# Attention over compacted tokens: when the first checks and loads run, and the order of the last product

## The chip, the core and the metric

The kernel runs on one core of a Trainium2 chip (trn2). The metric is device time in microseconds (us) of one execution, as the median of several runs. The engines are TensorE (PE, with its weight loads listed as PEld), VectorE (DVE), ScalarE (ACT), GpSimd (POOL) and SyncE (SP). In this kernel SP issues the plain transfers and POOL the indexed ones: gathers of token rows and scatters of result rows.

## The reference

The input `x` is 16 batches of 512 features by 1024 tokens, `mask` is 16 by 1024 of zeros and ones (about half are ones), `Wq` and `Wo` are 512 by 512.

```python
xt = transpose(x)                       # B, T, D
q = xt @ Wq.T                           # 8 heads of 64; queries are keys and values too
scores = scale * einsum('bhqd,bhkd->bhqk', qh, qh)
logits = (scores * cmask + (1.0 - cmask) * NEG) * rmask
attn = softmax(logits)
ctx = einsum('bhqk,bhkd->bhqd', attn, qh)
out = x + transpose(ctx @ Wo.T)
```

A token whose mask is 0 has a row of zero logits, so it attends to all tokens equally and its context is the mean of `q`. A token whose mask is 1 attends only to tokens whose mask is 1.

## The kernel before

The fast path works on compacted tokens. For each batch `slots` and `index` compute, from the mask, the list of the unmasked tokens, and POOL gathers their rows into `C` = 544 slots: four blocks of 128 (`xa`) and a tail of 32 (`xt`). The tails of some batches are collected, so that a group of batches shares one product for them. The masked tokens get one row per batch, the mean of `q` times `Wo`, added to their `x`.

Products that need more precision than one f16 are made of two halves. A value is scaled and split into `h` and `l` (f16), and three products `h*h`, `l*h`, `h*l` are added up. `xsplit` makes `xh` and `xl` of the transposed tokens, `split` makes `wqh`, `wql`, `woh`, `wol` of the weights, `qsplit` makes `hl` of the queries. `qsplit` then spreads these halves over the partitions by four SP transfers (L442 to L445) into `xx`, the operand of the scores.

For one batch the work is: transposes of the tokens (L398) and their splits (L358 ACT, L359 DVE); 8 query products (L421, four chunks `e` by two column halves `g`, 12 matmuls each) and their copies by ACT (L424); the spread into `xx`; transposed values (L467, L469); a shift for the exponentials, from the largest square norm of a head's queries (`top`, L505 to L511, and `bottom`, L518 to L532, whose result is `nm`); scores (L580, and L555 for the tails), exponentials on ACT (L584, L559), products with the values (L598, L601), a copy `c` (L605), reciprocal sums (L620 to L639) that go through DRAM and come back spread as `rb`, `norm` (L665 to L671) and the output product (L681). The result is added to the gathered rows (L686) and scattered by POOL (L765).

The sums of all tokens that the mean needs come from the natural layout. `load_half` (batches 0 and 1, 256 KB each) and `load_all` (the others, 512 KB each) load rows of `x_nat`, and `sum_half` (L343) sums them on ACT. For the first two batches the halves are put into buffers called `xm`, `ub` and `xi`.

The fast path is only valid for numbers in range. `range_x` (L366, one reduction for each chunk of `xh`, and L368) and `range_w` (L373, one reduction over all of `wqh` or `woh`) put the largest sizes into `big`, and `ranges` compares them at the end (L379 to L386). Nothing else reads them.

The order is set in two ways. `run` writes the program: a list `first` for the start of batch 0, then for each batch 18 steps of scores, between which a list `m` of other work (with costs that only set where an item goes) and lists `free` by step are laid. The framework then orders each engine's instructions when the program is built. `behind(i)` asks it to put what follows after instruction `i`. `once(dma, after)` makes a transfer wait for an instruction. Each engine, and each issuing queue, works through its own list in order. `self.st[0]["top"]` is the last reduction of the first shift (L523), that is, what the first exponentials of the kernel subtract. PSUM has two buffers for scores (`ps_s`), one for the values' product and two for everything else (`pm`).

`last` makes the output product of the last batch. Its three first chunks of features do not need the last `norm`; the fourth (`range(3, DC)`) does. `pos[0]` to `pos[3]` are the four blocks of 128 slots, `pos[4]` is the product of the tails.

Of the kernel before, what the change touches and what calls it, by code (L numbers as in the profile page):

```python
# [12 lines left out]
F16 = mybir.dt.float16  # L13
I32 = mybir.dt.int32
AF = mybir.ActivationFunctionType
ALU = mybir.AluOpType
AX = mybir.AxisListType
PS = bass.MemoryType.PSUM

P = 128  # L20
# [5 lines left out]
DC = D // P  # L26
# [5 lines left out]
CT = C - 512  # L32
# [17 lines left out]
class Fast:  # L50
# [78 lines left out]
    def setup2(self):  # L129
        nc, fixed = self.nc, self.fixed  # L130

        self.quad = fixed("quad", [P, HG])
        nc.vector.tensor_reduce(self.quad, self.ident.rearrange("p (r t) -> p r t", r=HG), AX.X, ALU.add)
        self.xh = fixed("xh", [P, DC, CQ], F16)
        self.xl = fixed("xl", [P, DC, CQ], F16)
        for t in (self.xh, self.xl):
            nc.gpsimd.memset(t[:, :, CM + 1:], 0.0)

        self.rcol = [fixed("rcol%d" % k, [P, P]) for k in range(2)]
        self.smcol = [fixed("smcol%d" % k, [P, P]) for k in range(2)]  # L140
        for t in self.rcol + self.smcol:
            nc.gpsimd.memset(t, 0.0)

        self.big = fixed("big", [P, self.B + 2])

        self.par = fixed("par", [P, 2])
        nc.vector.tensor_tensor(self.par, self.quad[:, 0:2], self.quad[:, 2:4], ALU.add)
# [194 lines left out]
        with self.behind(*self.exp):  # L342
            self.nc.scalar.activation(s["xm"][k], s["xm"][k], AF.Copy, accum_out=s["ms2"][:, k:k + 1])  # L343

    def load_all(self, b, c):

        t = self.sb([P, T], F32, "xm", 2)
        self.nc.sync.dma_start(out=t, in_=self.x_nat[b, c * P:(c + 1) * P, :])
        self.st[b]["xm"].append(t)

    def xsplit(self, dst, src, scaled=False):
# [15 lines left out]
        if c == DC - 1:  # L367
            nc.vector.tensor_reduce(self.big[:, b:b + 1], s["top4"], AX.X, ALU.max)  # L368

    def range_w(self, name):  # L370
        wh = self.w[name][0]
        k = self.B + "qo".index(name)
        self.nc.vector.tensor_reduce(self.big[:, k:k + 1], wh, AX.XY, ALU.max, apply_absolute_value=True)  # L373

    def ranges(self):

        nc, B = self.nc, self.B
        ok = self.sb([P, B + 2], F16, "okr")
        nc.vector.tensor_scalar(ok[:, :B], self.big[:, :B], XMAX, None, ALU.is_le)  # L379
        nc.vector.tensor_scalar(ok[:, B:], self.big[:, B:], WMAX, None, ALU.is_le)  # L380
        pe = self.pm([P, B + 2])
        nc.tensor.matmul(pe, lhsT=self.on16, rhs=ok, start=True, stop=True)
        least = self.sb([P, 1], F32, "okl")
        nc.vector.tensor_reduce(least, pe, AX.X, ALU.min)
        nc.vector.tensor_scalar(least, least, float(P), None, ALU.is_equal)
        nc.vector.tensor_scalar(self.ok, self.ok, least, None, ALU.mult)  # L386
# [388 lines left out]
    def last(self, b, todo):  # L775

        for f in self.soon + todo:
            f()
        self.soon = []
        while self.urgent or self.spare:  # L780
            self.issue()
        self.paced = False
        s = self.st[b]
        self.recip(b, 3)
        pos = []
        for i in range(2):
            t = self.ps_s.tile([P, 2, D], F32, tag="s", name="pss")
            pos += [t[:, k, :] for k in range(2)]
        pos.append(self.pm([P, D]))
        for i in range(4):  # L790
            self.product(s["ch"], s["cl"], slice(i * P, (i + 1) * P), pos[i], range(3))
        self.norm(b, 3)
        tails = slice(0, len(self.group[b]) * CT)
        self.product(*s["ct"], tails, pos[4], range(1))
        for i in range(4):
            if i == 2:
                self.product(*s["ct"], tails, pos[4], range(1, 3))
            self.project(b, i, pos[i], range(3, DC))
        self.project_tail(b, pos[4], range(3, DC))

    def run(self, flag):
        B = self.B
        L = lambda f, *a: lambda: f(*a)
# [5 lines left out]
        def xt(n):  # L809
            return [(0.45, L(self.xt, n, c)) for c in range(4)] + [(0.25, L(self.xt, n, 4))]  # L810

        def query(n, e, g):
            u = [(1.37, L(self.query, n, e, g))]
            return u + [(0, L(self.qsplit, n, e))] if g else u

        def value(n, e):
            return [(0.45, L(self.value, n, e))]
# [7 lines left out]
        tails, rests = {}, {}  # L825
# [39 lines left out]
        first = query(0, 0, 0) + xt(0)[3:] + [(0, L(self.facts, 0, 2))] + query(0, 1, 0) + query(0, 0, 1)  # L865
        first += [(0, index1)] + value(0, 0) + g1[:1] + query(0, 1, 1)[:1] + g1[1:2]
        first += [(0, L(self.split, "q", c, 1)) for c in range(DC)]
        first += [(0, lambda k=k: self.load_half(1, k, self.last_xt)) for k in range(2 * DC)]
        first += value(0, 1) + [(0, L(self.value_tail, 0, 0))] + query(0, 2, 0) + g1[2:3] + query(0, 2, 1)[:1] + g1[3:4]
        first += [(0, L(self.sum_half, 1, k)) for k in range(3)] + [(0, shift0)]  # L870
        for _, f in first:
# [1 line left out]
        with self.behind(self.st[0]["top"]):  # L873
            for _, f in query(0, 1, 1)[1:] + query(0, 2, 1)[1:]:
                f()
        self.paced = True
        begin = g1[4:] + [(1.5, lambda: None)] + query(0, 3, 0) + value(0, 2) + query(0, 3, 1) + value(0, 3)
        begin += [(0.3, L(self.value_tail, 0, 1)), (0, L(self.means, 0))]
        begin += [(0, L(self.load, "o", c)) for c in range(DC)]
        begin += [(0, L(self.range_x, 0, c)) for c in range(DC)] + [(0, L(self.range_w, "q"))]  # L880
        groups = [(g, min(h, B)) for g, h in ((2, 4), (4, 8), (8, 12), (12, 16)) if g < B]
        todo, ready, whole = [], [], []
        for b in range(B + 1):
            o, n = b - 1, b + 1
# [3 lines left out]
            free, early, late = {}, ([], []), []  # L888
# [13 lines left out]
            if n < B:  # L902
                m = xt(n)[:1] + early[0] + xt(n)[1:2] + chunk2 + xt(n)[2:3] + early[1] + xt(n)[3:] + tp + query(n, 0, 0) + query(n, 0, 1) + bt + value(n, 0)
# [13 lines left out]
            else:  # L917
# [7 lines left out]
                m = chunk2 + early[0] + early[1] + tp + bt + [(2.6, L(self.project_means, b))] + late + P_(0, 1, 2, 3)  # L925
# [3 lines left out]
                if b == g[0] - 2:  # L929
                    m.insert(7 if b == 0 else 0, (0.1, L(self.slots, *g)))  # L930
            if b == 1:
                m.append((0, L(self.range_w, "o")))
            if b == B - 1:
                m.append((0.1, self.ranges))
            if b == 0:
                m = begin + m
            if b + 2 < B:
                self.start(b + 2)
                for c in range(DC):
                    at = 3 * c + (0 if b else 4)  # L940
                    free.setdefault(at, []).append(L(self.load_all, b + 2, c))
                    free.setdefault(at + 4, []).append(L(self.sum_half, b + 2, c))
            if b == 0:
                for k in range(3, 2 * DC):
                    free.setdefault(k // 2, []).append(L(self.sum_half, 1, k))
            total = sum(c for c, _ in m)
            done, pos = 0.0, 0
            for st, (p, i) in enumerate(S):
# [20 lines left out]
                big = st >= 4 and [c >= 1 for c, _ in fill if c > 0.1][:1] == [True]  # L969
# [166 lines left out]
```

## Time and profile before

| | |
|---|---|
| Median of 3 runs | 1118.86 us (1118.13 to 1123.56) |
| Profiled execution, its own time | 1119.63 us |
| Its span, first to last instruction | 1117.8 us |
| PE / DVE / ACT / POOL busy | 1071.0 / 731.6 / 676.8 / 288.6 us |
| Mean granted TensorE clock | 0.996 |
| DMA, mean over the span | 162 GB/s |
| Idle before ACT's exponentials L584, for scores | 209.6 us |
| Idle before DVE's `norm` L665, for `rb` | 48.4 us |

The table is of one profiled execution, except its first row. Busy time of PE is modelled at the ends of matmuls, so it is somewhat too long. Idle time of an engine other than the one that sets the pace costs nothing; the prediction therefore goes to the stretches in which PE waits.

### The profile page before, as it was taken

Reading aid. Unit: us, or ns where it says so; the run is one execution under the profiler, and the core shown is the slowest. Engines: PE = TensorE matmul, PEld = TensorE weight load, DVE = VectorE, ACT = ScalarE, POOL = GpSimd, SP = SyncE. Lnnn points to the kernel's source line nnn. Section 1 sums busy time; section 2 is a strip of 40 time slices with the busy share of each in tenths; the row PEclk is TensorE's granted clock in tenths of the full one; section 3 lists DMA queues with packets and bytes.
Section 4 is the critical chain, followed back from the end, with each engine's and each line's share of the span. In section 5 each row is a group of like instructions: output and inputs, shape, how many; then the busy total and the mean of one; then the engine's idle time right before and its main releaser. Section 6 shows DMA issues by size and latency. Waiting matters only on the chain.

```text
span 1117.8 us, 23184 instructions
## 1 busy us (share of the span) xinstructions
PE 1071.0 (96%) x8386; PEld 697.7 (62%) x8386; DVE 731.6 (65%) x2369; ACT 676.8 (61%) x1716; POOL 288.6 (26%) x303
## 2 busy tenths in 40 slices
PE   7899999999999999999999999999999999998987
PEld 6576666666666666566666666666666666665543
DVE  6787466765665767667665766857576685655543
ACT  5876666666566666567565665666566666645540
POOL 3101031323202222222222232222222223214542
PEclk9999999999999999999999999999999999999999
DMA  7745455646546464565655566465656654546652
GB/s 235 212 121 155 128 164 150 190 127 185 144 128 177 125 209 142 163 179 159 192 145 173 158 185 182 130 193 146 198 157 176 185 146 146 147 115 194 187 168 72
DMA packets 78121, 181.34 MB, mean 162 GB/s; under 512 B 15008, under 2 KB 16800, under 8 KB 78000
## 3 DMA queue, kind: packets, MB, share of 16 engines
q1 hardware_dynamic: 56816, 111.62, 36.4%
q0 software_dynamic: 21184, 68.18, 19.2%
q8 instruction: 68, 1.11, 0.4%
q14 instruction: 53, 0.43, 0.1%
HBM read 92.34 MB, written 33.91 MB: 113 GB/s over the span
## 4 chain that ended last, share of the span: by engine, by line
PE 63%; DVE 14%; DMA 10%; issue 7%; ACT 3%; POOL 2%; SPq 1%; DVEq 0%; POOLq 0%; ACTq 0%
PE pav L598 17%; PE pss L580 16%; PE pm L681 13%; PE pm L421 8%; DMA xi<-x_in,idx 3%; DMA rb<-rd 2%; PE pm L398 2%; PE pav L601 2%; DMA rd<-rr 2%; ACT p L584 2%; POOL y_out L765 2%; PE pm L467 1%; DVE c L665 1%; PE pm L634 1%; DVE tmp L458 1%
## 5 line engine op out<-in xcount | busy, mean ns | idle before, releaser
L584 ACT ACTIVATE p<-pss,nm 128x544 f32<-128x544 f32 x512 | 363.8, 715 | 219.9 <-PE pss L580 209.6
L580 PE MATMUL pss<-xx 128*128 128x272 f16 x2048 | 303.1, 280 | 5.4 <-DMA xx<-hl 2.6
L598 PE MATMUL pav<-p,v 128*64 128x272 f32 x2048 | 278.9, 402 | 0.9 <-ACT c L605 0.9
L580 PEld LDWEIGHTS <-xx 128*128 128x128 f16 x2048 | 192.4, 99 | 85.2 <-issue 40.2
L598 PEld LDWEIGHTS pav<-p,v 128*64 128x64 f32 x2048 | 131.0, 136 | 98.2 <-issue 38.5
L765 POOL DMA_INDIRECT y_out<-xa,idx x68 | 70.9, 1043 | 304.8 <-PE pss L580 163.6
L421 PE MATMUL pm<-xh,wqh 128*128 128x274 f16 (+1 forms) x512 | 143.7, 281 | 0.1
L421 PE MATMUL pm<-xl,wqh 128*128 128x274 f16 (+1 forms) x512 | 143.2, 280 | 0.2 <-DVE xl L359 0.2
L421 PE MATMUL pm<-xh,wql 128*128 128x274 f16 (+1 forms) x512 | 143.2, 280 | 0.0
L313 POOL DMA_INDIRECT xa<-x_in,idx x68 | 69.3, 1020 | 181.7 <-PE pss L580 89.8
L421 PEld LDWEIGHTS <-wqh 128*128 128x128 f16 x1024 | 99.7, 99 | 23.1 <-issue 4.7
L584 ACT ACTIVATION_READ_ACCUMULATOR p<-pss,nm 128x1 f32 x512 | 102.9, 201 | 0.0
L686 DVE SCALAR_TENSOR_TENSOR xa<-pm,xa 128x512 f32<-128x512 f32 x60 | 41.4, 689 | 87.1 <-PE pm L681 87.0
L313 POOL DMA_INDIRECT xi<-x_in,idx x60 | 59.7, 995 | 145.7 <-PE pss L580 49.0
L424 ACT ACTIVATE q<-pm 128x272 f32<-128x272 f32 (+1 forms) x128 | 51.2, 400 | 69.0 <-PE pm L421 68.7
L681 PE MATMUL pm<-woh,ch 128*128 128x512 f16 x240 | 91.1, 380 | 1.0 <-DVE xa L686 1.0
L681 PE MATMUL pm<-woh,cl 128*128 128x512 f16 x240 | 91.0, 379 | 0.0
L681 PE MATMUL pm<-wol,ch 128*128 128x512 f16 x240 | 90.9, 379 | 0.0
L765 POOL DMA_INDIRECT y_out<-xi,idx x60 | 60.3, 1004 | 89.6 <-PE pss L580 70.6
L665 DVE TENSOR_TENSOR c<-c,rb 128x544 f32<-128x544 f32 x64 | 46.3, 724 | 54.7 <-DMA rb<-rd 48.4
L681 PEld LDWEIGHTS <-ch 128*128 128x128 f16 x480 | 46.3, 98 | 41.8 <-issue 1.2
L752 DVE TENSOR_TENSOR xi<-xi,ub 128x512 f32<-128x512 f32 (+1 forms) x60 | 40.1, 687 | 40.6 <-DMA xi<-x_in,idx 27.7
(191 smaller groups left out, 1584.7 us busy)
## 6 DMA issues: line engine op xcount, KB each, us to landing
xx<-hl SPq DMA_DIRECT2D x256, 136.0 KB
xm<-x_nat_in SPq DMA_DIRECT2D x56, 512.0 KB
rb<-rd SPq DMA_DIRECT2D x128, 136.0 KB
pt<-c SPq DMA_DIRECT2D x64, 136.0 KB
pt<-p SPq DMA_DIRECT2D x64, 136.0 KB
ub<-ud SPq DMA_DIRECT2D x16, 256.0 KB
xi<-x_nat_in SPq DMA_DIRECT2D x8, 256.0 KB
xa<-x_in,idx POOLq DMA_INDIRECT x68, 4.3
```

The lines of the kernel that those rows point to most:

```text
L313: dma = self.nc.gpsimd.indirect_dma_start(out=tile[:n], out_offset=None, in_=self.x, in_offset=bass.IndirectOffsetOnAxis(ap=idx, axis=0))
L398: self.pe = nc.tensor.transpose(pt[:, c, :], x[:n, c * P:(c + 1) * P], self.ident[:n, :n]).ins
L421: self.beat = nc.tensor.matmul(pq, lhsT=w[:, c, e * P:(e + 1) * P], rhs=xx[:, c, cols], start=(k == 0), stop=(k == 3 * DC - 1)).ins
L424: nc.scalar.activation(s["q"][:, e, cols], pq, AF.Copy, scale=1.0 / (SX * SW))
L580: self.beat = nc.tensor.matmul(pt[:, g, :CH], lhsT=xx[:, 2 * k, i * P:(i + 1) * P], rhs=xx[:, 2 * k + a, g * CH:(g + 1) * CH], start=(a == ...
L584: self.exp = [nc.scalar.activation(t.rearrange("p (g c) -> p g c", g=2), pt[:, :, :CH], AF.Exp, bias=s["nm"][p // HG][:, p % HG:p % HG + 1 ...
L598: nc.tensor.matmul(s["pav"][k * DK:(k + 1) * DK, g, :CH], lhsT=s["v"][p][:, i, k * DK:(k + 1) * DK], rhs=ps[k][:, cols], start=(i == 1), s ...
L665: nc.vector.tensor_tensor(c, c, s["rb"][p], ALU.mult)
L681: nc.tensor.matmul(po[:cols.stop - cols.start], lhsT=a[:, e, cols], rhs=w[:, e, :], start=(e == 0 and k == 0), stop=(e == DC - 1 and k == 2))
L686: self.nc.vector.scalar_tensor_tensor(x, po, 1.0 / (SX * SW), x, ALU.mult, ALU.add)
L752: self.nc.vector.tensor_tensor(x[:n], x[:n], s["ub"][:n], ALU.add)
L765: dma = self.nc.gpsimd.indirect_dma_start(out=self.out, out_offset=bass.IndirectOffsetOnAxis(ap=idx, axis=0), in_=x, in_offset=None)
```

## The change

The change moves work, and removes none.

- `range_x` of batch 0 and `range_w` of `Wq` are put behind the first shift. `range_w` now makes one reduction for each chunk of 512 columns instead of one for all four, so `big` and `ok` have six more columns.
- The halves 4 to 7 of batch 1 (four transfers of 256 KB), the four loads of `Wo` (256 KB each) and the first loads of batch 2 (512 KB each) wait for the first shift. Which step the sums of batch 1 are laid into changes with them (`k // 3` for `k // 2`).
- In `last`, the product of the tails is written behind the four blocks, not between them.

```diff
-        self.big = fixed("big", [P, self.B + 2])
+        self.big = fixed("big", [P, self.B + 2 * DC])
...
-    def load_all(self, b, c):
+    def load_all(self, b, c, after=None):
...
-        self.nc.sync.dma_start(out=t, in_=self.x_nat[b, c * P:(c + 1) * P, :])
+        self.once(self.nc.sync.dma_start(out=t, in_=self.x_nat[b, c * P:(c + 1) * P, :]), after)
...
-    def range_w(self, name):
-        wh = self.w[name][0]
-        k = self.B + "qo".index(name)
-        self.nc.vector.tensor_reduce(self.big[:, k:k + 1], wh, AX.XY, ALU.max, apply_absolute_value=True)
+    def range_w(self, name, c):
+
+        k = self.B + DC * "qo".index(name) + c
+        self.nc.vector.tensor_reduce(self.big[:, k:k + 1], self.w[name][0][:, c, :], AX.X, ALU.max, apply_absolute_value=True)
...
-        tails = slice(0, len(self.group[b]) * CT)
-        self.product(*s["ct"], tails, pos[4], range(1))
         for i in range(4):
-            if i == 2:
-                self.product(*s["ct"], tails, pos[4], range(1, 3))
             self.project(b, i, pos[i], range(3, DC))
-        self.project_tail(b, pos[4], range(3, DC))
+        self.project_tail(b, pos[4])
...
-        first += [(0, lambda k=k: self.load_half(1, k, self.last_xt)) for k in range(2 * DC)]
+        first += [(0, lambda k=k: self.load_half(1, k, self.last_xt)) for k in range(DC)]
...
+        first_top = self.st[0]["top"]
+
+        def apart(f, *a):
+            def run():
+                with self.behind(first_top):
+                    f(*a)
+            return run
...
-        begin += [(0, L(self.load, "o", c)) for c in range(DC)]
-        begin += [(0, L(self.range_x, 0, c)) for c in range(DC)] + [(0, L(self.range_w, "q"))]
+        begin += [(0, L(self.load, "o", c, None, first_top)) for c in range(DC)]
+        begin += [(0, apart(self.range_x, 0, c)) for c in range(DC)] + [(0, apart(self.range_w, "q", c)) for c in range(DC)]
...
-                m.append((0, L(self.range_w, "o")))
+                m += [(0, L(self.range_w, "o", c)) for c in range(DC)]
...
-                    free.setdefault(at, []).append(L(self.load_all, b + 2, c))
+                    free.setdefault(at, []).append(L(self.load_all, b + 2, c, None if b else first_top))
...
                 for k in range(3, 2 * DC):
-                    free.setdefault(k // 2, []).append(L(self.sum_half, 1, k))
+                    if k >= DC:
+                        free.setdefault(0, []).append(lambda k=k: self.load_half(1, k, first_top))
+                    free.setdefault(k // 3, []).append(L(self.sum_half, 1, k))
```

More of the change, by code (lines that the diff above doesn't have):

```diff
@@ L368, in range_x @@
             nc.vector.tensor_reduce(self.big[:, b:b + 1], s["top4"], AX.X, ALU.max)
-    def range_w(self, name):
-        wh = self.w[name][0]
-        k = self.B + "qo".index(name)
-        self.nc.vector.tensor_reduce(self.big[:, k:k + 1], wh, AX.XY, ALU.max, apply_absolute_value=True)
+    def range_w(self, name, c):
+        k = self.B + DC * "qo".index(name) + c
+        self.nc.vector.tensor_reduce(self.big[:, k:k + 1], self.w[name][0][:, c, :], AX.X, ALU.max, apply_absolute_value=True)
     def ranges(self):
         nc, B = self.nc, self.B
-        ok = self.sb([P, B + 2], F16, "okr")
+        ok = self.sb([P, B + 2 * DC], F16, "okr")
         nc.vector.tensor_scalar(ok[:, :B], self.big[:, :B], XMAX, None, ALU.is_le)
         nc.vector.tensor_scalar(ok[:, B:], self.big[:, B:], WMAX, None, ALU.is_le)
-        pe = self.pm([P, B + 2])
+        pe = self.pm([P, B + 2 * DC])
         nc.tensor.matmul(pe, lhsT=self.on16, rhs=ok, start=True, stop=True)
```

## The prediction

> **What bounds the kernel now.** I read the page first, then two-microsecond windows and the engines' timelines at the two places that the change touches: the start of batch 0 and the last product.
>
> ```profile
> PE 1071.0 (96%) x8386; PEld 697.7 (62%) x8386; DVE 731.6 (65%) x2369; ACT 676.8 (61%) x1716; POOL 288.6 (26%) x303
> ```
>
> TensorE is busy 96% of the span. Only its idle time, 47 us in all, can be won, and only where the change touches it. The windows (PE, PEld, DVE, ACT, POOL busy, clock, DMA share, GB/s) show where it idles near the start:
>
> ```profile
> 24.00:26.00 2.00, 1.73 (x16) 1.31 (x13) 2.00 (x5) 1.53 (x3) 0.74 (x1) 1.00 0.98 348
> 26.00:28.00 2.00, 1.01 (x5) 0.45 (x6) 2.00 (x5) 1.01 (x3) 0.94 (x1) 1.00 1.04 367
> 30.00:32.00 2.00, 0.93 (x8) 0.54 (x6) 2.00 (x2) 2.00 (x8) 1.24 (x2) 1.00 0.86 198
> 32.00:34.00 2.00, 0.62 (x4) 0.32 (x4) 0.61 (x3) 0.16 (x2) 0.64 (x1) 1.00 0.94 339
> 46.00:48.00 2.00, 0.93 (x7) 0.65 (x7) 2.00 (x5) 2.00 (x6) 0.00 (x0) 1.00 0.03 7
> ```
>
> DVE is full up to 32 while the DMA engines are full too; at 46 ACT and DVE are full and PE waits. VectorE's timeline names what fills it, and what comes behind (start, duration, line, output<-input, idle before):
>
> ```profile
> 22.36 0.71 DVE L366 TENSOR_REDUCE top<-xh 128x1 f32<-128x545 f16 x1
> 24.53 0.71 DVE L366 TENSOR_REDUCE top<-xh 128x1 f32<-128x545 f16 x1
> 26.83 1.34 DVE L366 TENSOR_REDUCE top<-xh 128x1 f32<-128x545 f16 x2
> 29.70 2.28 DVE L373 TENSOR_REDUCE big<-wqh 128x1 f32<-128x2048 f16 x1
> 32.45 0.15 DVE L507 TENSOR_TENSOR smcol<-smcol,sdt 128x4 f32<-128x4 f32 x1
> 35.80 0.16 DVE L520 TENSOR_SCALAR nm<-pm 128x4 f32<-128x4 f32 x1 [0.54 <-PE pm L518]
> ```
>
> The five range checks stand before the shift `nm` of the first exponential. The chain of waits, PE's and ACT's timelines show the second thing that is late, the spread query halves `xx`:
>
> ```profile
> 28.00 6.07 DMA xx<-hl
> 30.65 0.28 PE L421 MATMUL pm<-xh,wql 128*128 128x274 f16 x1
> 33.18 0.62 PE L580 MATMUL pss<-xx 128*128 128x272 f16 x4 [2.25 <-DMA xx<-hl]
> 34.20 0.62 PE L580 MATMUL pss<-xx 128*128 128x272 f16 x4 [0.40 <-DMA xx<-hl]
> 36.00 0.71 ACT L584 ACTIVATE p<-pss,nm 128x544 f32<-128x544 f32 x1 [3.83 <-DVE nm L520]
> ```
>
> The end is a row of five scatters on POOL, 1.2 to 1.3 us apart, then the last landing:
>
> ```profile
> 1106.20 0.96 POOL L765 DMA_INDIRECT y_out<-xa,idx  x1 [12.43 <-DVE xa L686]
> 1107.93 0.96 POOL L765 DMA_INDIRECT y_out<-xa,idx  x1 [0.78 <-DVE xa L686]
> 1109.23 0.96 POOL L765 DMA_INDIRECT y_out<-xa,idx  x1 [0.35 <-DVE xa L686]
> 1110.50 0.90 POOL L765 DMA_INDIRECT y_out<-xg,tails  x1 [0.31 <-issue]
> 1111.71 0.96 POOL L765 DMA_INDIRECT y_out<-xa,idx  x1 [0.30 <-issue]
> ```
>
> **The change, part by part.** I take the order on each engine from the two built programs, and durations from the rows.
>
> *Checks off VectorE.* The four L366, L368 and L373 leave the stretch 22-32. The first two L366 stand where other waits cover part of them: squares end on ACT at 25.52, so `sd` (L459) moves from 26.01 only to 25.55. From there the chain value-transpose, L487, L492 moves by 0.5; L373 goes whole, so L507 comes at about 29.7 instead of 32.45. On PE the two small products for the shift (L509, L518) now stand among the last query matmuls, not behind the eight score matmuls: L511 about 30.2, L520 about 31.0 (before 35.80), the "first largest score" L523 about 31.4 (36.20).
>
> *Loads behind that score.* Four of the eight 256 KB halves of batch 1 (k 4 to 7), the four `wo` loads (256 KB each) and the first 512 KB loads of batch 2 wait on SP for L523. So `xx` of chunk 0 has 1.05 MB less ahead of it: 3.0 us at the 348 to 367 GB/s of 24-28. Its first spread can issue at 25.3 (25.91), the fourth about 27.4. When does it land? The row says 6.07 us from issue. [...] I take 30.0, since half of the backlog goes and the DMA share stays near 1 till then.
>
> *First scores.* Then PE's own matmuls end last: scores start at 31.1 and PE has these eight, L509 and L518 behind it at 32.0 instead of 35.62: **-3.6 us**. ACT must first do the query copy L424 and `corr`, so the first exponential is at 32.1 instead of 36.00.
>
> *From there to batch 1's first query (58.92).* New: two sums of halves (k 4, 5; L343, pitch 0.61) stand on ACT ahead of the fourth exponential, and their transfers are issued at 31.6 and 32.2. With two gathers, 1.05 MB at 350 GB/s, they land about 35.5. Queued behind them on ACT is the exponential that frees a score buffer for PE: **+1.8** (1.2 if landed early, 2.5 if late). Gone: the old waits at 38.9 and 39.65, 0.22 and 0.40. Also the four splits of `wo` (L162, pitch about 0.53, 2.1 us) leave ACT before 49, where PE waited 0.53, 0.56 and 0.37 for exponentials: I count **-1.3** of these 1.46. Sum of the start: -3.6 + 1.8 - 0.6 - 1.3 = **-3.7 us**. Bounds: 5.8 if all 2.2 us of later idle time goes too; 1.7 if `xx` lands at 33.4 and the lead at the first scores is all there is. [...]
>
> *What is moved later and costed at nothing.* The spreads of chunk 1 wait behind two halves on SP, but their data is ready at 33.1 (38.07) and PE needs them about 38; they land about 37.8. The checks of `xh` and `wq` fall in DVE's idle stretches after 33 (2.51 idle before 41.61); each L373 becomes four, 0.63 each by L366's pitch, so 0.3 us more a weight, 0.6 in all. The `wo` splits (L163), its checks and ACT's L162 move to 55-75, where DVE had waits of 1.03, 0.73, 0.41, 0.97 and 0.78 and ACT one of 2.93, while PE ran without a gap. If that cover is gone, up to 2 us come back. `wo` is first multiplied at 116.83. POOL's order is untouched but for the last two scatters; its `xt` gather merely starts earlier. From 60 to the tail the order is the same and PE nearly full, so the lead is carried to the end.
>
> *The tail.* With the tails' product last, the first output block needs no three tail matmuls ahead (0.77 us): its addition is at 1104.4 (1105.23), its scatter at 1105.4 (1106.20). PE waits for no one, so POOL sets the pace: four more at 1.26 give 1110.4 for the last (1111.71). The tail addition is ready at 1109.7, hidden by 0.7. The last scatter carries 64 rows, not 128: another 0.3 by the 274 GB/s of 1113-1114. Together **-1.6** (0.8 if only the first scatter moves, 2.0 at most).
>
> Sum: -3.7 - 1.6 = -5.3. Against the profiled execution's 1119.63 this gives 1114.3. The median is 0.77 lower, so I predict **1113.6**, or -0.47%.
>
> **The rivals.**
>
> *The lead is lost at ACT.* The sums wait for halves that now come late, and exponentials queue behind them. For it: ACT had not a gap from 36 to 54. Against: DMA is nearly idle from 44 to 48 and only 1 MB is ahead. If it eats 2 to 3.5 of the 3.7, the tail and a rest remain: 1115.6 to 1117.1.
>
> *All idle time goes.* ACT, relieved, runs ahead and the later waits vanish: -5.8 (my upper bound) to -6.8 (all that the windows show idle from 22 to 58) at the start: 1110.5 to 1111.5. Against: the new ACT wait is in the program's order.
>
> *Slower: `wo` comes too late.* Its loads now stand on SP behind the spreads of chunks 1 to 3 and the `pt` copies. ACT's L162 stands between exponentials of batch 0 and would block them, and VectorE's L163 blocks `nm` of the second half. I expect SP to issue `wo` about 45.5 to 47.5, landed by 50, and L162 reached at 57. It decides from a landing at 57; each microsecond later costs PE one: beyond 62 the kernel is slower than before, beyond 68 by over 0.5%. At 69 it stands at 1125. Against: seven microseconds of margin.
>
> That the change does nothing is excluded at the tail, where the order plainly differs.
>
> **How the numbers follow.** Forecast 0.66, own range 1111.6 to 1115.6; ACT loses the lead 0.17; all idle goes 0.09; slower 0.08. One half of a percent, 5.6 us, is about what a measurement can tell from no change: the line is at 1113.3, almost through my forecast. Faster: 0.30 of the forecast plus 0.09 = 0.39. Same: 0.36 plus 0.17 = 0.53. Slower 0.08. Range 1110.5 to 1118.1: from the second rival's end to the whole lead lost with the tail at its lower bound (1118.86 - 0.8); the slower rival is left out.
>
> **What would show it.** Right: L520 near 31, first L580 near 31 with no wait for `xx`, first L584 near 32, batch 1's first L421 near 55, the last scatter carrying `xg`, some 5 us before 1111.71. Wrong: a wait for `xx` still ending after 33, an ACT wait for `xi` over 3 us, an ACT or DVE wait for `wo`, or a lead at 60 that has gone by 120.

## The result, and the profile after

The changed kernel took 1115.4 us (median of 18 runs, 1109.8 to 1118.9) beside 1121.1 us for the kernel before on the same chip: ratio 0.995, 95% interval 0.9934 to 0.9965, which is 5.6 us less. Predicted were 5.3 us less: 1113.6, counted from 1118.86 for the kernel before; in these runs that kernel itself took 2.2 us more. A second series of the same kernel gave 0.9939 (0.9918 to 0.996).

The profiled execution took 1115.95 us with a span of 1114.2. The page, VectorE's timeline at the first shift, PE's at the first scores, ScalarE's from the first exponential, and SP's issues there (start, duration, line, output<-input, idle before and its releaser):

```profile
PE 1071.4 (96%) x8386; PEld 699.1 (63%) x8386; DVE 732.3 (66%) x2375; ACT 676.9 (61%) x1716; POOL 290.8 (26%) x303
```
```profile
31.64 0.16 DVE L507 TENSOR_TENSOR smcol<-smcol,sdt 128x4 f32<-128x4 f32 x1
33.05 0.16 DVE L520 TENSOR_SCALAR nm<-pm 128x4 f32<-128x4 f32 x1 [0.48 <-PE pm L518]
```
```profile
32.99 1.09 PE L580 MATMUL pss<-xx 128*128 128x272 f16 x8
36.92 0.29 PE L555 MATMUL pss<-xx 128*32 128x272 f16 x2
40.35 0.28 PE L555 MATMUL pss<-xx 128*32 128x272 f16 x1 [2.88 <-DMA xx<-hl]
```
```profile
34.03 0.71 ACT L584 ACTIVATE p<-pss,nm 128x544 f32<-128x544 f32 x1
37.27 0.63 ACT L343 ACTIVATE xi<-xi 128x512 f32<-128x512 f32 x1 [0.45 <-DMA xi<-x_nat_in]
39.20 0.63 ACT L343 ACTIVATE xi<-xi 128x512 f32<-128x512 f32 x1 [1.20 <-DMA xi<-x_nat_in]
39.82 0.69 ACT L584 ACTIVATE p<-pss,nm 128x544 f32<-128x544 f32 x1
```
```profile
33.67 0.91 SPq L337 DMA_DIRECT2D xi<-x_nat_in  x2
35.20 0.47 SPq L442 DMA_DIRECT2D xx<-hl  x1
35.76 0.55 SPq L443 DMA_DIRECT2D xx<-hl  x1
```

These times can't be set beside those of before as they stand. The first query matmul of the second block, which the change doesn't reach, came at 19.93 us before and at 21.72 here. It is taken as the zero below. On that scale the shift L520 moved from 15.9 to 11.3, the first exponential from 16.1 to 12.3, and the 2.25 us that PE waited for `xx` at its first scores are gone. A new wait stands 7 us behind the first scores: the third L555, the first matmul to read chunk 1 of `xx`, waits 2.88 us. The windows (PE, PEld, DVE, ACT, POOL busy, clock, DMA share, GB/s) show it, with the DMA engines full, and show the later waits closed:

```profile
32.00:34.00 2.00, 2.00 (x17) 1.57 (x18) 1.20 (x8) 1.64 (x7) 0.72 (x2) 1.00 0.33 89
38.00:40.00 2.00, 0.00 (x0) 0.00 (x0) 1.69 (x3) 0.81 (x3) 0.00 (x0) 1.00 1.01 238
46.00:48.00 2.00, 2.00 (x17) 1.30 (x16) 1.78 (x8) 2.00 (x7) 0.00 (x0) 1.00 0.37 83
```

The end, on POOL:

```profile
1102.29 0.96 POOL L765 DMA_INDIRECT y_out<-xa,idx  x1 [11.55 <-DVE xa L686]
1106.09 0.96 POOL L765 DMA_INDIRECT y_out<-xa,idx  x1 [0.31 <-issue]
1107.36 0.91 POOL L765 DMA_INDIRECT y_out<-xg,tails  x1 [0.31 <-issue]
```

The last product's L634 is at 1095.63 before and 1092.59 after. From it the last scatter's issue comes at 14.77 (16.08 before), the end of the span at 21.7 (22.2).

**One profile doesn't measure this change.** Fourteen profiles were taken in all. Three readings sum most of each: from the zero to batch 1's first exponential (ScalarE's order of exponentials is the same in all, and in the table's seven the same matmuls stand ahead of it), from there to the last exponential, and from L634 to the end.

| kernel | zero at | start | middle | tail | wait for `xx` |
|---|---|---|---|---|---|
| before | 19.93 | 77.1 | 994.3 | 22.2 | 2.25 |
| before, again | 22.87 | 77.8 | 993.2 | 22.2 | 2.18 |
| new tail alone (old start) | 21.94 | 80.0 | 990.1 | 21.0 | 3.54 |
| changed | 21.72 | 73.1 | 993.4 | 21.7 | 2.88 |
| changed, again | 22.29 | 74.1 | 994.1 | 21.4 | 2.14 |
| head alone (old tail) | 21.87 | 73.3 | 990.1 | 22.2 | 2.17 |
| tails fourth (new start) | 22.24 | 74.4 | 989.8 | 21.9 | 2.50 |

The zero itself varies by 3.6 us over the fourteen (19.93 to 23.53) and the middle by 5.6 (989.8 to 995.4), without any order by kernel. What varies in the middle is the clock and PE's waits: less the clock time that was lost there (1.7 to 6.8 us) and PE's idle time (19.9 to 25.1), 964.4 to 966.3 us are left in all fourteen. The start falls from 78.3 (mean of three) to 73.7 (mean of four): 4.6 us. The tail falls from 22.2 to a mean of 21.4 over the eight profiles that have the new one: 0.8 us. Together 5.4, close to the 5.6 of the runs.

### The profile page after: what moved, and what is told of

Read it like the earlier page. It is cut to its first block, busy times and chain, and to the rows that moved or that the text cites. A ratio compares the mean times of both kernels' runs of the same rounds, so it can differ in the third digit from the quotient of the medians.

```text
span 1114.2 us, 23190 instructions
## 1 busy us (share of the span) xinstructions
PE 1071.4 (96%) x8386; PEld 699.1 (63%) x8386; DVE 732.3 (66%) x2375; ACT 676.9 (61%) x1716; POOL 290.8 (26%) x303
## 4 chain that ended last, share of the span: by engine, by line
PE 66%; DVE 15%; DMA 8%; issue 6%; POOL 2%; ACT 2%; SPq 0%; POOLq 0%; DVEq 0%; ACTq 0%
PE pav L598 18%; PE pss L580 16%; PE pm L681 14%; PE pm L421 8%; DMA xi<-x_in,idx 3%; DMA rb<-rd 3%; PE pm L398 2%; PE pav L601 2%; PE pm L467 2%; DVE c L665 2%; DMA rd<-rr 2%; POOL y_out L765 1%; PE pm L634 1%; DVE hl L436 1%; DVE tmp L458 1%
## 5 line engine op out<-in xcount | busy, mean ns | idle before, releaser
L598 PEld LDWEIGHTS pav<-p,v 128*64 128x64 f32 x2048 | 131.5, 137 | 99.3 <-issue 40.7
L421 PE MATMUL pm<-xh,wqh 128*128 128x274 f16 (+1 forms) x512 | 143.7, 281 | 0.1
L421 PE MATMUL pm<-xl,wqh 128*128 128x274 f16 (+1 forms) x512 | 143.2, 280 | 0.2 <-DVE xl L359 0.2
L421 PE MATMUL pm<-xh,wql 128*128 128x274 f16 (+1 forms) x512 | 143.2, 280 | 0.0
L421 PEld LDWEIGHTS <-wqh 128*128 128x128 f16 x1024 | 99.6, 99 | 23.3 <-issue 4.9
L424 ACT ACTIVATE q<-pm 128x272 f32<-128x272 f32 (+1 forms) x128 | 51.2, 400 | 67.6 <-PE pm L421 67.1
```

What stands on the lines that cost most here:

```text
L421: self.beat = nc.tensor.matmul(pq, lhsT=w[:, c, e * P:(e + 1) * P], rhs=xx[:, c, cols], start=(k == 0), stop=(k == 3 * DC - 1)).ins
L424: nc.scalar.activation(s["q"][:, e, cols], pq, AF.Copy, scale=1.0 / (SX * SW))
L598: nc.tensor.matmul(s["pav"][k * DK:(k + 1) * DK, g, :CH], lhsT=s["v"][p][:, i, k * DK:(k + 1) * DK], rhs=ps[k][:, cols], start=(i == 1), s ...
```

## The experiments

### The parts by themselves

The tail alone, on the kernel before:

```diff
-        tails = slice(0, len(self.group[b]) * CT)
-        self.product(*s["ct"], tails, pos[4], range(1))
         for i in range(4):
-            if i == 2:
-                self.product(*s["ct"], tails, pos[4], range(1, 3))
             self.project(b, i, pos[i], range(3, DC))
-        self.project_tail(b, pos[4], range(3, DC))
+        self.project_tail(b, pos[4])
```

> Only the last product is changed: the tails' twelve matmuls and their scatter come last; the start is as before. Measured in the profile from the last product's first normalisation (L634) to the end of the span (22.17 us before, 21.61 after) and to the last scatter's issue (16.08 and 14.77). Theory: the last scatter is issued 1.3 us sooner, but its 64 rows land later than 128 rows did, so that only 0.5 to 0.7 us are left at the end: 0.3 to 0.8 us off the time. The prediction's own step (fewer rows land 0.3 us sooner): 1.6 us off. The start (from the first L421 of the second query block to batch 1's first L421, 38.99 us before) stays within 0.5.

Measured: 0.9985 (0.9967 to 1.0003), 1.7 us less, with an interval from 0.3 us more to 3.7 less. The last scatter is issued 14.76 after L634, the end is at 21.0. Over all eight profiles with the new tail the end comes at 20.9 to 21.8, 0.8 us sooner in the mean: the theory's upper end, half of the prediction's step. The start didn't stay within 0.5: the same instructions took 3 us longer than in the first profile of before. PE's timeline tells why:

```profile
36.48 2.16 PE L580 MATMUL pss<-xx 128*128 128x272 f16 x8 [3.54 <-DMA xx<-hl]
38.43 0.42 PE L509 MATMUL pm<-ident,smcol 128*128 128x128 f32 x1
41.06 0.43 PE L421 MATMUL pm<-xh,wqh 128*128 128x272 f16 x1
42.56 0.28 PE L421 MATMUL pm<-xh,wqh 128*128 128x272 f16 x1
```

After a wait of 3.54 us the eight score matmuls take 2.16 us instead of 1.09, and a query matmul 0.43 instead of 0.28, until 42.5: the granted clock is 0.50 there. It fell after shorter waits in other runs, and not after all of them; see the last section.

The checks alone (`apart` and the four parts of `range_w` as in the change):

```diff
-        begin += [(0, L(self.range_x, 0, c)) for c in range(DC)] + [(0, L(self.range_w, "q"))]
+        begin += [(0, apart(self.range_x, 0, c)) for c in range(DC)] + [(0, apart(self.range_w, "q", c)) for c in range(DC)]
```

> Only the range checks are moved behind the first shift and cut in four; loads, sums and the tail are as before. Theory: the checks carry most of the gain of the start. The shift is ready some 4.5 us sooner, but the spread halves of chunk 0 still land at 33.2 (1.5 us behind PE), so the first exponential comes at 33.7 to 34.2 instead of 36.0; the later waits at 46 to 50 (1.46 us) stay; the start stretch is 36.8 to 37.6 us (before 38.99, after 36.16). Rival, the loads carry the gain, since the transfers are then simply the next thing that is late: within 0.7 us of before, 38.3 or more.

Measured: 0.9951 (0.9929 to 0.9972). Batch 1's first L421 comes at 37.0, as expected, but ten matmuls fewer than in the kernel before stand ahead of it (16 fewer with the loads alone, below), so this reading can't be compared. By batch 1's first exponential, ahead of which the matmuls are the same, the start is 76.4 (78.3 in the mean of before). The shift is as early as in the whole change (L520 at 11.3), and then PE waits for `xx` twice, as expected. The first exponential comes at 13.2, sooner than the 13.8 to 14.3 that were expected.

```profile
34.89 0.62 PE L580 MATMUL pss<-xx 128*128 128x272 f16 x4 [1.12 <-DMA xx<-hl]
36.73 1.07 PE L580 MATMUL pss<-xx 128*128 128x272 f16 x4 [1.21 <-DMA xx<-hl]
```

The loads alone, with the sums as in the change:

```diff
-        first += [(0, lambda k=k: self.load_half(1, k, self.last_xt)) for k in range(2 * DC)]
+        first += [(0, lambda k=k: self.load_half(1, k, self.last_xt)) for k in range(DC)]
...
-        begin += [(0, L(self.load, "o", c)) for c in range(DC)]
+        begin += [(0, L(self.load, "o", c, None, first_top)) for c in range(DC)]
...
-                    free.setdefault(at, []).append(L(self.load_all, b + 2, c))
+                    free.setdefault(at, []).append(L(self.load_all, b + 2, c, None if b else first_top))
...
+                    if k >= DC:
+                        free.setdefault(0, []).append(lambda k=k: self.load_half(1, k, first_top))
```

> Only loads are moved (batch 1's halves 4 to 7, the output weight, batch 2's first chunks) behind the first largest score, and the sums of halves as in the change; checks and tail are as before. Theory: alone they gain nothing, since the shift is still late (L520 at 35.8) and the loads behind it then come later still, at 36.3, with ACT waiting for them some 2 to 4 us: the start stretch is 38.5 to 41 us (before 38.99). Rival, loads carry the gain: 37.5 or less.

Measured: 0.9955 (0.9934 to 0.9975). This theory fell: alone the loads gain as well, with batch 1's first exponential at 75.2. `xx` is in time, so the scores no longer hold the shift's two small products up behind them, and the shift comes at 14.0 instead of 15.9 although all checks still stand in front of it:

```profile
30.80 1.35 PE L580 MATMUL pss<-xx 128*128 128x272 f16 x8
32.79 0.30 PE L509 MATMUL pm<-ident,smcol 128*128 128x128 f32 x1 [0.64 <-DVE smcol L507]
```

The head, both together (the first diff of this section taken back in the changed kernel):

> The whole change but for the last product, which is as before. Theory: the start stretch is that of the changed kernel, 36.2 us within 0.4 (before 38.99), the tail that of before, 22.2 within 0.3; the time is 2 to 4.5 us below before. If the 2.0 us by which the profiled middle of the changed kernel was shorter belongs to the change, it shows here and not with the tail alone; if it is chance, it differs between these four kernels with no order.

Measured: 0.9929 (0.9904 to 0.9953), 8.0 us less, beside 5.5 and 5.0 us for its parts and 5.6 for the whole change. With intervals of about 2.5 us to each side these times don't tell whether the parts add, and don't show what the tail is worth. The first exponential does tell: it comes at 16.1 after the zero in the first profile of before (15.9 in the second), at 13.2 with the checks alone, at 14.2 with the loads alone and at 12.3 with both. That is 2.8, 1.9 and 3.8 us sooner, so the parts don't add. Shift and `xx` are two waits of one stretch; either removed shows the other. The two starts of 76.4 and 75.2 say less, since with the checks alone the clock was at half for 6.8 us of the start (0.50 from 36 to 42), and with the loads alone at 1.00 from 12 to 22 and from 34 to 52. The middle of 990.1 was had with the old start too, so it doesn't belong to the change.

The two kernels once more, unedited:

> The changed kernel once more, unedited, to see what an unchanged program's profile varies by. Read against the first L421 of the second query block as zero: batch 1's first exponential (L584) came 77.1 us later in before, 80.1 in the kernel with only the last product changed (the same program up to there) and 73.1 and 73.3 in the changed kernel and in its head alone; from there to the last exponential 994.3, 990.1, 993.4 and 990.1. Theory: the start of the changed kernel repeats within 0.6 us, since no transfer that varies ends a wait before the third L555; the middle differs by up to 4 us without any edit. Rival, the middle of 993.4 belongs to the new tail's kernel: it repeats within 0.5.

> The kernel before once more, unedited, for the spread of its own profile. Theory: its start varies by more than the changed kernel's, since the spread halves of chunk 0 end a wait there (2.25 and 3.54 us in two profiles of the same start): batch 1's first exponential 76.5 to 80.5 after the zero (changed kernel 73.1 to 74.5); the tail repeats within 0.1 of 22.2 us from L634 to the end. Rival, the 80.1 of the one profile was an outlier: 77.1 within 0.5.

Measured: the changed kernel's start came at 74.1, 1.0 later, which is more than the 0.6 expected; its wait was shorter (2.14), but the clock fell after it (0.50 from 42 to 44). The middle was within 0.7, but at 994.1 no shorter than before's. Before was measured equal to itself, 1.0003 (0.9985 to 1.0021); its start came at 77.8, its tail at 22.2.

### The wait that took the place of the old ones

Two things end near 40 us: the spreads of chunk 1 land, and ScalarE gets past the sums of the token halves. First the sums of halves 4 to 7 two steps later:

```diff
-                    free.setdefault(k // 3, []).append(L(self.sum_half, 1, k))
+                    free.setdefault(k // 3 if k < DC else k // 2 + 1, []).append(L(self.sum_half, 1, k))
```

> The changed kernel with ScalarE's sums of batch 1's halves 4 to 7 moved two steps later, so that the fourth exponential no longer waits for these halves; all loads stay. Theory that the spread halves of chunk 1 are what PE waits for (their bytes stand behind the token halves): the wait at the third L555 stays at 2.2 to 3 us and batch 1's first exponential comes at 72.6 to 73.3 after the zero (73.1 in the changed kernel). Theory of the prediction, ScalarE's wait for the halves: the wait goes and it comes at 70.5 to 71.5.

Measured: 0.9952 (0.9933 to 0.9971), start 72.4. Between the two theories: the wait fell to 1.10 us, but the matmul that waits came no sooner (18.2 after the zero, 17.9 to 18.6 in the four profiles of the changed start). PE only did other work first, since the fourth exponential was there.

```profile
40.72 0.28 PE L555 MATMUL pss<-xx 128*32 128x272 f16 x1 [1.10 <-DMA xx<-hl]
```

So the landing ends the wait, and ScalarE hid what PE could have done meanwhile. Then the loads one step later as well:

```diff
-                        free.setdefault(0, []).append(lambda k=k: self.load_half(1, k, first_top))
+                        free.setdefault(1, []).append(lambda k=k: self.load_half(1, k, first_top))
```

> As the run before, and batch 1's halves 4 to 7 are also loaded one step later, behind the spreads of chunk 1. Theory of the spread halves: without 0.5 MB of token halves in front, chunk 1 lands 1.5 to 2 us sooner, the wait at the third L555 falls from 2.9 to at most 1.4 us and batch 1's first exponential comes at 71 to 72 us; 1 to 2 us off the time. Theory of ScalarE's wait: no better than the run before. A third way, that the gathers of batch 1 fill the queues instead: the wait stays above 2.

Measured: 0.9951 (0.9934 to 0.9969), start 72.7, the third L555 at 18.4. The step didn't do what it was meant to: on SP two halves still stood in front of the spreads (issued at 34.95, the first spread at 36.49), so this run repeats the one before. A dependency on the last L437 (chunk 2's, kept as `self.halves`) does it, and holds the loads of `wo` and of batch 2's first chunks in the same way:

```diff
-        first_top = self.st[0]["top"]
+        first_top, first_halves = self.st[0]["top"], self.halves
...
-                        free.setdefault(0, []).append(lambda k=k: self.load_half(1, k, first_top))
+                        free.setdefault(0, []).append(lambda k=k: self.load_half(1, k, first_halves))
```

> The run halves_late left the order on SP as it was. Here the loads that the change holds back (batch 1's halves 4 to 7, the output weight, batch 2's first chunks) wait for the last operation on chunk 2's query halves instead of the first largest score, so that all of them stand behind the spreads of chunks 1 and 2; the sums are two steps later, as in sums_late. The third L555 came 17.9 to 18.6 us after the zero in six profiles of the changed head, whatever the sums did. Theory that the token halves in front delay chunk 1's spreads: it comes at 16.0 to 17.2, the wait falls below 0.7 us, batch 1's first exponential at 71 to 72. Rival, the spreads are late because their data is (L436 ends 13.5 after the zero) and the gathers of batch 1 share the engines: 17.7 or more, no gain over sums_late (72.5).

Measured: 0.9963 (0.9944 to 0.9981). SP's and PE's timelines:

```profile
36.89 0.46 SPq L442 DMA_DIRECT2D xx<-hl  x1
41.98 1.95 SPq L337 DMA_DIRECT2D xi<-x_nat_in  x4
```
```profile
48.18 0.66 PE L398 MATMUL pm<-ident,xa 128*128 128x128 f32 x4 [0.46 <-DVE tmp L487]
49.39 0.65 PE L398 MATMUL pm<-ident,xa 128*128 128x128 f32 x4 [0.56 <-DVE xl L359]
50.49 0.66 PE L398 MATMUL pm<-ident,xa 128*128 128x128 f32 x4 [0.44 <-DVE xl L359]
51.55 0.62 PE L580 MATMUL pss<-xx 128*128 128x272 f16 x4 [0.41 <-ACT p L584]
```

The first spread is issued 13.48 us after the zero, as in the changed kernel (35.20 less 21.72), and the third L555 runs at 16.9 without a wait. So half a megabyte of token halves in front of them on SP's queue cost chunk 1's spreads at least 1.0 to 1.8 us (1.3 and 1.55 beside the two runs with the same sums). That part of the theory held. The start did not follow: 72.9, no better than with the sums alone, though four matmuls fewer stand ahead of that reading. The halves' sums now stand among the splits of batch 1's tokens at 47 to 50, and PE waits 1.87 us there, where the changed kernel has no wait.

The other way round, chunk 1's data sooner: its split (L435 to L437) is not held behind the first shift.

```diff
+        for _, f in query(0, 1, 1)[1:]:
+            f()
         with self.behind(self.st[0]["top"]):
-            for _, f in query(0, 1, 1)[1:] + query(0, 2, 1)[1:]:
+            for _, f in query(0, 2, 1)[1:]:
                 f()
```

> The changed kernel with the split of chunk 1's query halves (L435 to L437) no longer behind the first shift: it goes into VectorE's time before it, and its spreads stand ahead of the token halves on SP. Price: 1.2 us of VectorE in front of the shift, of which some 0.9 fill waits that are there; first exponential at 12.3 to 13.2 after the zero (12.3 before). Theory that chunk 1's data and its place in the queue make the third L555 late: it comes at 15.0 to 16.5 with no wait over 0.5, batch 1's first exponential at 71 to 72.5 (73.1 to 74.5 in the changed kernel). Rival, ScalarE's sums of halves 4 and 5 then hold the exponentials and PE instead: 73 or more.

Measured: 0.995 (0.9931 to 0.9968). The third L555 came at 15.2 without a wait, as the theory said, and the first exponential at 12.0, a little sooner than it said. Then the rival decided: the start is 76.1. Half 5, now behind the spreads, landed late, ScalarE's sum waited 2.85 us for it in front of the query copy L424, and PE behind that:

```profile
42.57 0.63 ACT L343 ACTIVATE xi<-xi 128x512 f32<-128x512 f32 x1 [2.85 <-DMA xi<-x_nat_in]
```
```profile
43.63 0.39 PE L421 MATMUL pm<-xh,wqh 128*128 128x274 f16 x1 [3.38 <-ACT q L424]
```

This is ScalarE held by halves that come late, as in the prediction's +1.8 and its first rival; here nothing else holds PE. Both remedies together:

> Both of the two runs before together: chunk 1's split ahead of the shift, and the loads and the sums of halves 4 to 7 later. Theory: neither transfer nor ScalarE holds PE in the stretch 15 to 19 after the zero; batch 1's first exponential at 70 to 71.5, the time 1 to 3 us below the changed kernel's. Rival, the wait moves on to the sums, which must be done before batch 1's queries, or to the output weight: 72.5 or more.

Measured: 0.9941 (0.9918 to 0.9964), start 72.7. In this run and the one before, six matmuls more than in the changed kernel stand ahead of that reading, some 0.7 us by their rows there, so that the start lies between theory and rival. The wait is the rival's: PE has no wait over 0.3 us from 31 to 51, then one for the split of batch 1's tokens, which on ScalarE stands behind a sum that waited 2.00 us for its half.

```profile
48.05 0.63 ACT L343 ACTIVATE xi<-xi 128x512 f32<-128x512 f32 x1 [2.00 <-DMA xi<-x_nat_in]
51.03 0.66 PE L398 MATMUL pm<-ident,xa 128*128 128x128 f32 x4 [1.25 <-DVE xl L359]
```

None of the five is told apart from the changed kernel by its time, and none is shown to beat it.

### The tail

The tails' product and scatter fourth of five:

```diff
         for i in range(4):
+            if i == 3:
+                self.project_tail(b, pos[4])
             self.project(b, i, pos[i], range(3, DC))
-        self.project_tail(b, pos[4])
```

> The changed kernel with the tails' product and scatter placed fourth of five, before the last full block. Zero is the last product's L634. The changed kernel issues its last scatter at 14.8 us and ends at 21.6, the kernel with the new tail alone at 14.8 and 21.1; before 16.1 and 22.2. Theory that 64 rows land later than 128: the last full scatter is issued at 14.8 and ends 6.1 us later, at 20.8 to 21.1, 0.3 to 0.8 below the changed kernel's end. Theory that POOL or the block products set the end: the scatters come later by the tails' 2.6 us of matmuls on PE, the last at 15.5 or more, the end at 21.6 or more.

Measured: 0.9956 (0.994 to 0.9972), last scatter 15.24 after L634, end at 21.9.

```profile
1104.86 0.90 POOL L765 DMA_INDIRECT y_out<-xg,tails  x1 [0.73 <-issue]
1106.07 0.96 POOL L765 DMA_INDIRECT y_out<-xa,idx  x1 [0.30 <-issue]
```

My theory that 64 rows land later fell. The last scatter here has 128 rows, and the span still ends 6.6 us after its issue. In the five profiles with the old tail this stretch is 6.1 us, in the eight with the new one 6.2 to 7.0 (mean 6.7), whichever start they have. Counted from the first scatter's issue the end comes 11.6 us later in the five, 11.2 to 12.0 (mean 11.7) in the eight: what the tail gained, 0.8 us, is what its first scatter gained (issued 9.70 after L634, 10.57 before), and not what its last one gained (1.31). What makes the stretch after the last issue longer and unsteady stays open: the transfers that the windows show end 8 to 10 us after the first scatter's issue in all of them, with the new tail in a trickle of 8 to 29 GB/s.

## Why the prediction was right, and where not

- **Checks off VectorE.** Predicted L507 at 29.7 and L520 at 31.0. With the 1.79 us of the late zero taken off: 29.85 and 31.26. Right.
- **Loads behind the score; first scores.** Predicted 31.1 without a wait for `xx`, the first exponential at 32.1; measured 31.2 and 32.2. Right. The loads-alone run shows that the loads ahead of `xx` were the reason: it came in time with the checks still there. That it had landed by 31.2 excludes 33.4, about what the row's 6.07 us from an issue near 27.4 gives. The 30.0 that the forecast used was my estimate, and no run shows it: the runs show only that the first scores didn't wait for `xx`, at 31.2 here and at 30.80 (zero 20.0) with the loads alone. What POOL's gathers cost it was not shown either, since no run took them away.
- **From there to batch 1's first query: the step that was mis-sized.** I put +1.8 on ScalarE's wait for the halves, and chunk 1's spreads at nothing, "PE needs them about 38; they land about 37.8". ScalarE did wait, 1.65 us. But PE asked for chunk 1 already at 35.7 and got it at 38.6 (both less 1.79): 2.88 us where I had 1.8. I had the readiness right (33.1, issued at 33.4); I missed that the third L555 is the first reader, and that the halves ahead would cost the spreads over a microsecond.
- **The later waits.** -1.3 of 1.46 counted; PE has no wait over 0.2 between 40.7 and 60. Right, a little better.
- **The sum of the start**, -3.7. By batch 1's first L421 it is -2.8 in the first pair of profiles, whose starts both ran at full clock, and -3.3 in the means; by its first exponential -4.0 and -4.6. The -2.8 is what the steps above add to: 1.1 worse in one step, 0.2 better in another. The stretch from that L421 to the exponential, before and after, is beyond what I summed:

```profile
58.92:96.98 38.06, 37.13 (x324) 26.36 (x323) 26.66 (x108) 25.68 (x65) 5.32 (x5) 1.00 0.60 164
57.88:94.81 36.93, 36.17 (x324) 26.17 (x323) 31.56 (x118) 27.59 (x69) 5.07 (x5) 1.00 0.62 169
```

PE idles 0.9 us there before and 0.8 after, but the same matmuls take 37.1 us before and 36.2 after, and so they do in the other profiles of the two starts. Their order is another; what makes it the quicker one stays open. And in two of the three profiles of the old start the wait for `xx` was followed by microseconds at half the clock (0.50 from 36 to 42 with the new tail alone, from 38 to 40 in the second profile of before), where I had assumed full clock throughout. That the changed kernel's new wait was followed by the same in three of four profiles (0.50 from 42 to 44, in the head alone from 40 to 42) was not foreseen either.
- **Moved later at no cost.** ScalarE reached `wo` at 59.77 without waiting, so the slower rival didn't come near (the first product with `wo` was at 116.67 before, not at 116.83):

```profile
59.77 0.62 ACT L162 ACTIVATE woh<-xa 128x512 f16<-128x512 f32 x1
```

- **The tail: wrong in size.** The pace was as predicted: the last scatter 1.31 us sooner. "Another 0.3" for 64 rows had the wrong sign; the stretch after the last issue grew by 0.5 in the mean, so that 0.8 of 1.6 us were left. That is the lower bound that the prediction gave for the case that only the first scatter moves.

So it was in part luck that 5.3 us came out close to 5.6: the tail was 0.8 too high, and the start 0.3 too low in the first pair and 0.9 in the means, by terms that were not in the sum. With starts that differ by up to 3 us between profiles of one program, the second figure is a rough one.

## What to carry to other kernels

Two waits of one stretch don't add: find out by taking each away alone, and expect the next transfer in the same queue to be the new bound. When a transfer is moved behind an event, look at the first instruction that reads what is issued right after it, in the order of the engine that reads, and not at the mean need. When two programs are compared from one instruction to another, count the work ahead of it: a reading moves when the order of the program does. For a change of half a percent a pair of profiles shows which wait moved, but not how much it is worth: here the part of the span that no edit touched varied as much as the effect.

## What the runs showed of the hardware

PE's granted clock fell to half after waits of about 2 us, in some executions and not in others. In the stretch that the change touches it fell to 0.50 after 2.14, 2.17, 2.18, 2.50, 3.38 and 3.54 us, and stayed at 1.00 after 2.25 and 2.88, and after 1.10, 1.25 and 1.36; with the checks alone it fell to 0.50 (from 36 to 42) after two waits of 1.12 and 1.21 with 0.6 us of work between. The changed kernel, second profile, after its wait of 2.14 us:

```profile
38.00:40.00 2.00, 0.04 (x1) 0.00 (x0) 2.00 (x4) 1.83 (x7) 0.53 (x1) 1.00 1.00 274
40.00:42.00 2.00, 1.82 (x11) 1.25 (x12) 1.88 (x5) 0.35 (x1) 0.00 (x0) 0.73 0.94 268
42.00:44.00 2.00, 2.00 (x18) 0.84 (x16) 0.92 (x2) 0.00 (x0) 0.00 (x0) 0.50 0.97 300
44.00:46.00 2.00, 2.00 (x15) 1.05 (x15) 1.04 (x3) 1.79 (x5) 0.00 (x0) 0.92 0.02 5
```

The three windows with a lower clock lose (0.27 + 0.50 + 0.08) x 2 = 1.7 us of full clock, nearly as much as the wait. In the changed kernel's first profile the wait was longer, 2.88 us, and the clock stayed at 1.00:

```profile
36.00:38.00 2.00, 1.47 (x12) 0.90 (x10) 2.00 (x5) 1.55 (x6) 1.50 (x1) 1.00 1.00 311
38.00:40.00 2.00, 0.00 (x0) 0.00 (x0) 1.69 (x3) 0.81 (x3) 0.00 (x0) 1.00 1.01 238
40.00:42.00 2.00, 1.62 (x13) 1.31 (x14) 0.59 (x1) 1.37 (x4) 0.00 (x0) 1.00 1.02 254
42.00:44.00 2.00, 2.00 (x25) 1.06 (x25) 2.00 (x6) 1.06 (x3) 0.00 (x0) 1.00 0.91 266
```

So the length of a wait alone doesn't tell here whether the clock falls. What decides it was not shown.

The late zero goes with the clock too. In twelve of the fourteen profiles the granted clock was at 0.50 for a while between 14 and 22 us, in the first profile of before and in that of the loads alone it was 1.00 throughout that stretch. In these two the zero is at 19.9 and 20.0. In the eight whose windows from 14 to 22 us lose 1.7 us of full clock it is at 21.7 to 22.8, in the four that lose 3.3 to 3.4 at 22.9 to 23.5.
